# Query and key projections by seven half products in place of eight, block sums on GpSimd, filler steps laid out anew

## The chip, the core and the metric

The kernel runs on one core of one Trainium2 chip. The metric is the device time of one execution, in microseconds. A core has TensorE (PE, matmuls into the PSUM), VectorE (DVE), ScalarE (ACT), GpSimd (POOL) and a queue processor SP that issues transfers; they run beside each other and wait for each other by semaphores. In the profile PEld is TensorE's weight load, which overlaps its matmuls.

## The reference

Causal self-attention with 16 heads of 32 channels, a normalisation, a mixture of eight experts of which each token uses one, and a second normalisation:

```python
Q, K, V = x @ W_Q.T, x @ W_K.T, x @ W_V.T          # x: 8 x 1024 x 512
attn = Q K^T / sqrt(32), causal; probs = softmax(attn)
x = layernorm(x + (probs @ V) @ W_O.T)
probs = softmax(x @ router_w.T + router_b)          # 8 experts
y = (x @ expert_w[top1].T + expert_b[top1]) * max(probs)
out = layernorm(x + y)
```

All inputs are float32 and are multiplied as float32.

## The kernel before

**Rounds and steps.** The 16 heads are taken in groups of four (128 channels) and the eight sequences one after another, which makes 32 rounds (`n`; sequence `b = n // 4`, group `g = n % 4`). A round has nine steps (`u`). In each step TensorE does, in this order: the scores of one block of queries and keys for four heads (`exps`, lines 745 and 751); one unit of "maxima" for the round that is one and a third ahead (`maxima`, line 635: score blocks from which VectorE takes each row's extreme at line 645); a filler; small extra matmuls, where there are any; and the values (`values`, line 787: probabilities times V). ScalarE turns the scores into exponentials (line 757) and, as room allows, takes the exponentials that give each row its sum (`exp_sums`, line 687). GpSimd cuts the diagonal blocks of the probabilities (line 761, `affine_select`), at steps 0, 1, 2, 4 and 6 of a round: two in steps 1, 2 and 4, one in 0 and 6. The values of a step need that.

**Fillers.** A filler is a projection: 512 input channels in four chunks of 128, each times four groups of 32 output channels, into one PSUM bank. Each round needs four of them for the queries and keys of round `n + 2` (`project_qk`, two halves of the sequence times two matrices, line 572), and four others: output projections of the previous sequence (`output`, line 842), or value projections of the next one (`project_v`, line 600), or, for the first sequence, small products for the router. Nine steps have eight fillers, so one of the other four is cut in two halves of two chunks (`in_halves`), with a copy out for each half: fillers stand in steps 0 to 8, with the halves in steps 5 and 7 (`HALVES_AT`). In a half step the fourth maximum is taken only after the filler was copied out.

**Order.** All engines' orders are written out by hand, instruction by instruction. VectorE's order in a step is: the maxima; one entry of the list `later`, if there is one; the filler's copy out (line 579, 581, 595 or 823); a fourth maximum that was left; the copies of the extras; the addition of the values to the context (lines 803 and 807); statistics of a finished output row block (lines 830, 831). `later` holds the normalisations of the first layer norm (`normalize`, line 858, 128 x 512 elements read and written in SBUF, followed by a store of `x1` on SP) and the two additions that finish a sequence's router logits (lines 936 and 937). Four normalisations follow each half sequence of output projections, which fill the first and second rounds of the next sequence; so they stand in steps 0 to 3 of the second round, and in steps 0, 2, 3 and 4 of the third, whose step 1 has the logits.

**Banks.** Of the eight PSUM banks one (`ps_f`) holds the filler and then the first head's scores of the next step, three (`ps_s`) hold the other heads' scores, and four (`ps_m`) go round among four maxima, extras and values. So the next scores wait for the filler's copy out.

**Inputs.** A sequence's x, transposed, stands in SBUF in two tiles of 512 tokens. The next sequence's tiles are loaded at step 7 of the second round (`load_x`, line 537), once the last reader is through. SP issues these loads, the fetches of h (x again, for the residual, line 815) and the stores of `x1` (line 861) in one queue. At the start the query weights and the first tile come in four chunks each, then the whole of the key weights, then the second tile.

**After the rounds.** Routing sorts tokens by expert, in small pieces of VectorE and GpSimd work (line 289 on GpSimd for the first six sequences, in rounds 26 to 30), and the experts follow, some 312 us.

The queries are scaled when they are copied out:

```python
                    if name == "wq":
                        nc.vector.tensor_scalar_mul(dst[n][:, cols], ps, -scale)
                    else:
                        nc.vector.tensor_copy(dst[n][:, cols], ps)
```

## Time and profile before

| what | value |
|---|---|
| median of three executions | 2213.53 us (2211.68 to 2213.75) |
| the profiled execution | 2210.15 us, its span 2208.1 us |
| TensorE, VectorE, ScalarE, GpSimd busy | 97%, 72%, 70%, 17% of the span |
| lead-in before the first round | 83.8 us |
| a round of sequences 1 to 5 | 57.31 to 57.74 us |
| one query or key projection on TensorE | 3.46 us to the next operation |
| granted TensorE clock | 0.997 |

The span is the time from the first to the last instruction of the profiled execution; some 2 us lie around it. A group's row names the line, engine and operation, output and inputs with their shapes, the number of instructions, then busy time and the mean of one in nanoseconds, then the idle time just before and what ended it. A timeline's row gives start and duration in microseconds, and in brackets the idle time before and its releaser; a matmul of float32 appears as two records.

### The profile page before, as it was taken

To read this page: it belongs to the slowest core of one execution; us is meant where nothing else is said; L and a number is where in the kernel's file an instruction comes from. 1 tells how busy PE (TensorE), PEld (TensorE's weight loads), DVE (VectorE), ACT (ScalarE), POOL (GpSimd) and SP (SyncE) were. 2 spreads that over 40 slices of the span, in tenths; PEclk is the share of its full clock that TensorE was granted. 3 is DMA by queue.
4 is the path that set the end of the run, shared out by engine and by line. 5 is a ranking of instruction groups with operands and counts; after the bars stand their busy time and mean duration, and the time that the engine had idled before them with its cause. 6 is when DMAs were issued, how large, how long until landed. Compare 5 with 4: busy or idle time off the path is not lost. (4 is left out here: it accounts for less than half of the span.)

```text
span 2208.1 us, 52961 instructions
## 1 busy us (share of the span) xinstructions
PE 2146.4 (97%) x20731; PEld 846.0 (38%) x20731; DVE 1581.3 (72%) x4867; ACT 1544.1 (70%) x2979; POOL 370.8 (17%) x485
## 2 busy tenths in 40 slices
PE   8998999999999999999999999999999988999998
PEld 2333333333333333333333333333333333344444
DVE  4666667766777677766776677667778876478766
ACT  2688777777777777887777877777777777243443
POOL 0000001100100010100110001001000224255554
PEclk9999999999999999999999999999999999999999
DMA  3001000110011002100120002000101031343432
GB/s 115 1 1 64 1 2 16 63 40 1 10 70 40 2 2 73 45 2 1 35 83 1 2 35 82 2 2 35 54 7 44 11 120 64 133 153 124 134 127 84
DMA packets 45736, 103.82 MB, mean 47 GB/s; under 512 B 5998, under 2 KB 5998, under 8 KB 45360
## 3 DMA queue, kind: packets, MB, share of 16 engines
q1 hardware_dynamic: 33456, 65.02, 8.3%
q0 software_dynamic: 11360, 35.40, 5.1%
q8 instruction: 164, 2.69, 0.5%
q14 instruction: 84, 0.69, 0.1%
q10 hardware_dynamic: 672, 0.02, 0.0%
HBM read 66.87 MB, written 35.39 MB: 46 GB/s over the span
## 5 line engine op out<-in xcount | busy, mean ns | idle before, releaser
L757 ACT ACTIVATE p<-s 128x512 f32<-128x512 f32 x584 | 558.5, 1009 | 422.8 <-PE s L751 422.7
L687 ACT ACTIVATE raw<-raw,low 128x1024 f32<-128x1024 f32 (+7 forms) x1024 | 779.1, 770 | 43.2 <-DVE low L645 43.2
L645 DVE CUSTOM_DVE_ANT_0 raw<-m,wide_mask 128x512 f32<-128x512 f32 (+3 forms) x1024 | 566.8, 587 | 156.0 <-PE m L635 156.0
L572 PE MATMUL f<-big 128*32 128x512 f32 x3968 | 451.4, 595 | 0.7 <-ACT p L757 0.7
L761 POOL TENSOR_SCALAR_AFFINE_SELECT p<-p 128x512 f32<-128x512 f32 x256 | 158.8, 638 | 1427.3 <-ACT p L757 1427.2
L645 DVE CUSTOM_DVE_ANT_0 raw<-m,wide_mask,lowA 128x256 f32<-128x256 f32 (+3 forms) x512 | 275.2, 548 | 136.2 <-PE m L635 136.2
L787 PE MATMUL pv<-p,V 128*32 128x512 f32 (+3 forms) x3072 | 304.0, 488 | 15.9 <-POOL p L761 5.6
L751 PE MATMUL s<-big 32*128 32x512 f32 (+3 forms) x3072 | 313.1, 487 | 0.0
L635 PE MATMUL m<-big 32*128 32x512 f32 (+3 forms) x3072 | 312.6, 486 | 0.3 <-DVE ctx L803 0.3
L435 PE MATMUL y<-big,gT 128*128 x568 | 255.8, 593 | 2.6 <-ACT gT L427 2.6
L600 PE MATMUL f<-big 128*32 128x512 f32 x2048 | 235.9, 596 | 4.2 <-ACT p L757 4.2
L572 PEld LDWEIGHTS f<-big 128*32 128x32 f32 x3968 | 116.2, 109 | 284.8 <-issue 222.6
L842 PE MATMUL f<-wo,ctx 128*32 128x512 f32 x1920 | 221.1, 596 | 2.6 <-ACT p L757 2.6
L635 PEld LDWEIGHTS m<-big 32*128 32x128 f32 x3072 | 171.7, 185 | 85.9 <-issue 59.0
L687 ACT ACTIVATION_READ_ACCUMULATOR raw<-raw,low 128x1 f32 x1024 | 200.1, 195 | 0.0
L807 DVE TENSOR_TENSOR ctx<-pv,ctx 128x512 f32<-128x512 f32 (+2 forms) x256 | 150.7, 589 | 38.6 <-PE pv L787 37.6
L787 PEld LDWEIGHTS pv<-p,V 128*32 128x32 f32 x3072 | 93.9, 110 | 188.7 <-issue 141.2
L751 PEld LDWEIGHTS s<-big 32*128 32x128 f32 x3072 | 142.8, 185 | 19.1 <-issue 14.6
L745 PE MATMUL s<-mT,ones_b 3*128 3x512 bf16 (+3 forms) x1536 | 134.0, 327 | 12.7 <-DVE mT L712 3.8
L435 PEld LDWEIGHTS y<-big,gT 128*128 128x128 f32 x568 | 102.4, 190 | 105.8 <-issue 101.9
L453 ACT ACTIVATE yrstd<-ymv,eps 128x1 f32<-128x1 f32 x71 | 20.9, 295 | 152.4 <-DVE ymv L451 134.5
L745 PEld LDWEIGHTS <-ones_b 3*128 3x128 bf16 x1536 | 46.5, 91 | 202.2 <-issue 190.7
(205 smaller groups left out, 1603.6 us busy)
## 6 DMA issues: line engine op xcount, KB each, us to landing
h<-in_x SPq DMA_DIRECT2D x64, 256.0 KB, 3.6
x<-h SPq DMA_DIRECT2D x64, 256.0 KB, 2.0
big<-in_xT SPq DMA_DIRECT2D x15, 1024.0 KB, 7.3
big<-in_ewT SPq DMA_DIRECT2D x8, 1024.0 KB
bias<-in_eb SPq DMA_DIRECT2D x1, 2048.0 KB
g<-x,r_gat POOLq DMA_INDIRECT x71
out<-g,r_sca POOLq DMA_INDIRECT x71
big<-in_xT SPq DMA_DIRECT2D x4, 256.0 KB, 5.7
```

The source lines that it names most:

```text
L435: nc.tensor.matmul(y_ps, lhsT=gT[:, k, :], rhs=big[:, bass.ds(e, 1), k, :].rearrange("p a o -> p (a o)"), start=(k == 0), stop=(k == NK - 1),)
L572: nc.tensor.matmul(ps, lhsT=w_sb[name][:, k, g * P : (g + 1) * P][:, m], rhs=xT_sb[b, c][:, k, :], start=start, stop=stop,)
L600: lambda ps, k, m, start, stop: nc.tensor.matmul(ps, lhsT=xT_sb[b, c][:, k, o : o + P][:, m], rhs=w_sb["wv"][:, k, :], start=start, stop=stop,
L635: nc.tensor.matmul(tiles[h][:, at : at + c1 - c0], lhsT=Q[n][r, qt * P : (qt + 1) * P], rhs=K[n][r, c0:c1], start=True, stop=True,)
L645: nc.vector.tensor_tensor_reduce(out=raws[n, h][:, to : to + w], in0=tiles[h][:, at : at + w], in1=wide_mask[:, 640 - w :] if last else wi ...
L687: nc.scalar.activation(a[:, to : to + w], a[:, to : to + w], AF.Exp, scale=-1.0, bias=low[n][:, qt, h : h + 1], accum_out=sums[n][:, qt, h ...
L745: nc.tensor.matmul(tiles[h][:, at : at + w], lhsT=ones_b[r, :], rhs=mT[n][r, q0 : q0 + w], start=True, stop=False,)
L751: nc.tensor.matmul(tiles[h][:, at : at + w], lhsT=K[n][r, j * P : (j + 1) * P], rhs=Q[n][r, q0 : q0 + w], start=False, stop=True,)
L757: nc.scalar.activation(p[:, hs], scores, AF.Exp, scale=-1.0)
L761: nc.gpsimd.affine_select(out=p[:, :, at : at + P], in_=p[:, :, at : at + P], compare_op=ALU.is_ge, fill=0.0, base=0, pattern=[[0, HG], [1 ...
L787: nc.tensor.matmul(ps[h * HD : h * HD + HD, parts[c][1] - w : parts[c][1]], lhsT=V[b, j][:, ch : ch + HD], rhs=p[:, h, at : at + w], start ...
L842: lambda ps, k, m, start, stop: nc.tensor.matmul(ps, lhsT=ctx_of(b * NG + k, qt * P, P)[:, m], rhs=w_sb["wo"][:, k, :], start=start, stop= ...
```

## The change

Half of the input channels of x and of the two weight matrices make a 2 x 2 problem: x has two halves of the sequence by two halves of the channels, the weights two halves of the channels by the two matrices. Strassen's method (in Winograd's form) does it with seven products of half the channels in place of eight, and sums of blocks.

- The class `seven` holds a round's products. GpSimd makes the sums of x blocks (`s`, 128 x 1024) and of weight blocks (`t`, 128 x 256), in one buffer each that is rewritten in place: `begin` after step 5 of the round before, `second` behind step 0, `third` behind step 1 and `fourth` behind step 3; `third` also adds two finished blocks (128 x 512). GpSimd stays in program order, so selects of later steps stand behind the sums.
- Products stand in steps 0 (two), 1, 2 (two), 3 and 5, the whole other fillers in steps 4, 6, 7 and 8. The second product of a step takes a bank of `ps_m`. They are copied or added into Q and K by VectorE, eight instructions of 128 x 512 in a round where there were four; the other fillers are not cut any more, which takes one copy out away.
- Rounds 0 and 1 are projected as before; then GpSimd scales both weight matrices in SBUF by the square root of the scale, once, in the lead-in.
- Short steps are now 1, 3 and 5; small extra matmuls move to steps 3 and 5; the next sequence's load moves to step 3 of the second round, after `fourth`.
- The first weights are loaded by columns: those of the first group before the first tile, the others after the second.
- `mT` (the turned maxima) has one buffer in place of two, the second half's context six in place of seven, and round 30 takes the buffer of `s` for its context.

```diff
-            def load_w(name, w, k0=0, k1=NK):
+            def load_w(name, w, o0=0, o1=D):
...
+                def sum(self, out, a, op, b):
+                    nc.gpsimd.tensor_tensor(out, a, b, op)
+
+                def begin(self):
+                    (a11, a12), (a21, a22) = self.x
+                    (b11, b12), (b21, b22) = self.w
+                    self.sum(self.s, a21, ALU.add, a22)
+                    self.sum(self.t[0], b12, ALU.subtract, b11)
+                    self.sum(self.t[1], b22, ALU.subtract, self.t[0])
+
+                def second(self):
+                    self.sum(self.s, self.s, ALU.subtract, self.x[0][0])
+                    self.sum(self.t[0], self.t[1], ALU.subtract, self.w[1][0])
+
+                def third(self):
+                    self.sum(self.s, self.x[0][1], ALU.subtract, self.s)
+                    self.sum(self.k[1], self.k[1], ALU.add, self.q[1])
+                    self.sum(self.t[1], self.w[1][1], ALU.subtract, self.w[0][1])
+
+                def fourth(self):
+                    self.sum(self.s, self.x[0][0], ALU.subtract, self.x[1][0])
+
+                def product(self, x, w, out):
+                    def mm(ps, k, m, start, stop):
+                        nc.tensor.matmul(ps, lhsT=w[:, k][:, m], rhs=x[:, k, :], start=start, stop=stop)
+
+                    return project(mm, out, ks=range(2))
...
+                    return {
+                        0: [self.product(self.s, self.t[0], copy(k[1])), self.product(a11, b11, copy(q[0]))],
+                        1: [self.product(self.s, self.t[1], add((q[1], q[0])))],
+                        2: [
+                            self.product(a12, b21, add((q[0], q[0]))),
+                            self.product(a22, self.t[0], add((q[1], q[1]), op=ALU.subtract)),
+                        ],
+                        3: [self.product(self.s, b22, add((k[0], k[1])))],
+                        5: [self.product(self.s, self.t[1], add((q[1], q[1]), (k[1], k[1])))],
+                    }, {0: self.second, 1: self.third, 3: self.fourth}
...
-            HALVES_AT = (NU - 4, NU - 2)
+            HALVES_AT = (1, 3, 5)
+            WHOLE_AT = (4, 6, 7, 8)
...
-                mT[n] = small.tile([P, S], BF16, tag="mT", bufs=2, name=f"mT_{n}")
+                mT[n] = small.tile([P, S], BF16, tag="mT", bufs=1, name=f"mT_{n}")
...
-            CTX_BUFS = (NG + 1, NG + 3)
+            CTX_BUFS = (NG + 1, NG + 2)
...
+            load_w("wq", wqT, 0, P)
             for k in range(NK):
                 load_x(0, 0, k, k + 1)
-                load_w("wq", wqT, k, k + 1)
-            load_w("wk", wkT)
+            load_w("wk", wkT, 0, P)
             load_x(0, 1)
+            load_w("wq", wqT, P, D)
+            load_w("wk", wkT, P, D)
...
+                if t == 2 * NC:
+
+                    nc.gpsimd.tensor_scalar_mul(w_sb["wq"], w_sb["wq"], -math.sqrt(scale))
+                    nc.gpsimd.tensor_scalar_mul(w_sb["wk"], w_sb["wk"], math.sqrt(scale))
+                    made_next = seven(2)
+                    made_next.begin()
...
+                made = {u: [f] for u, f in zip(range(HALF, NU) if n == NP - 1 else WHOLE_AT, fill)}
+                behind = {}
                 if n + 2 < NP:
...
+                    halves, behind = made_next.steps()
+                    made.update(halves)
...
+                    if u in behind:
+                        behind[u]()
...
+                    if u == HALVES_AT[-1] and n + 3 < NP:
+                        made_next = seven(n + 3)
+                        made_next.begin()
```

More of the change, by code (lines that the diff above doesn't have):

```diff
@@ L489, in attention @@
             pool2 = lambda name, bufs: st2.enter_context(tc.tile_pool(name=name, bufs=bufs))
-            vp, prob = pool2("v", 1), pool2("prob", 2)
+            vp, prob, sums_p = pool2("v", 1), pool2("prob", 2), pool2("sums", 1)
             NG = NH // HG
@@ L527, in attention @@
             xT_sb, Q, K, V, H, MV, ctxT, mT = {}, {}, {}, {}, {}, {}, {}, {}
-            def load_w(name, w, k0=0, k1=NK):
+            def load_w(name, w, o0=0, o1=D):
                 nc.sync.dma_start(
-                    out=w_sb[name][:, k0:k1], in_=w.rearrange("(k p) o -> p k o", p=P)[:, k0:k1]
+                    out=w_sb[name][:, :, o0:o1], in_=w.rearrange("(k p) o -> p k o", p=P)[:, :, o0:o1]
                 )
@@ L583, in project_qk, with __init__, steps, add @@
                 return project(mm, out)
+            class seven:
+                def __init__(self, n):
+                    b, g = divmod(n, NG)
+                    cols = slice(g * P, (g + 1) * P)
+                    self.x = [[xT_sb[b, c][:, k : k + 2, :] for k in (0, 2)] for c in range(NC)]
+                    self.w = [[w_sb[name][:, k : k + 2, cols] for name in ("wq", "wk")] for k in (0, 2)]
+                    self.s = sums_p.tile([P, 2, 512], F32, tag="s", name=f"xs_{n}")
+                    self.t = [sums_p.tile([P, 2, P], F32, tag=f"t{i}", name=f"ws_{n}_{i}") for i in range(2)]
+                    q, k = big[:, 5 + n % 3, 0:2], big[:, 5 + n % 3, 2:4]
+                    Q[n], K[n] = [a.rearrange("p k t -> p (k t)") for a in (q, k)]
+                    self.q, self.k = [q[:, c] for c in range(NC)], [k[:, c] for c in range(NC)]
+                def sum(self, out, a, op, b):
[19 more added lines that the diff above has]
+                    return project(mm, out, ks=range(2))
+                def steps(self):
+                    (a11, a12), (a21, a22) = self.x
+                    (b11, b12), (b21, b22) = self.w
+                    q, k = self.q, self.k
+                    def add(*to, op=ALU.add):
+                        def out(ps):
+                            for dst, a in to:
+                                nc.vector.tensor_tensor(dst, a, ps, op)
+                        return out
+                    def copy(dst):
+                        return lambda ps: nc.vector.tensor_copy(dst, ps)
+                    return {
[8 more added lines that the diff above has]
+                    }, {0: self.second, 1: self.third, 3: self.fourth}
@@ L796, in add @@
                     for c, (w, end) in parts.items():
-                        if (n, c) not in ctxT:
+                        if (n, c) == (NP - 2, 1):
+                            if (n, c) not in ctxT:
+                                ctxT[n, c] = sums_p.tile([P, 2, 512], F32, tag="s", name="ctx_more")[:, 0]
+                        elif (n, c) not in ctxT:
                             ctxT[n, c] = cp.tile([P, 512], F32, tag=f"ctx{c}", bufs=CTX_BUFS[c], name=f"ctx_{n}_{c}")
@@ L983, in attention @@
                 b, g = divmod(n, NG)
-                fill = []
-                if n + 2 < NP:
-                    fill += [project_qk(n + 2, c, name) for c in range(NC) for name in ("wq", "wk")]
                 if b == B - 1 and g < NG - 1:
                     first_qt, end_qt = ((0, HALF), (HALF, HALF + 2), (HALF + 2, NQT))[g]
-                    todo = [(output, b - 1, qt) for qt in range(first_qt, end_qt)]
+                    fill = [output(b - 1, qt) for qt in range(first_qt, end_qt)]
                 elif g < 2:
-                    todo = [(output, b - 1, qt) for qt in range(g * HALF, (g + 1) * HALF) if b]
-                    if not b:
-                        fill += [f for k in range(g * 2, g * 2 + 2) for f in router_of_ctx(k)]
+                    if b:
+                        fill = [output(b - 1, qt) for qt in range(g * HALF, (g + 1) * HALF)]
+                    else:
+                        fill = [f for k in range(g * 2, g * 2 + 2) for f in router_of_ctx(k)]
                 elif b + 1 < B:
-                    todo = [(project_v, b + 1, i) for i in range((g - 2) * HALF, (g - 1) * HALF)]
+                    fill = [project_v(b + 1, i) for i in range((g - 2) * HALF, (g - 1) * HALF)]
                 else:
-                    todo = [(output, b, qt) for qt in range(HALF)]
-                if len(fill) + len(todo) == NU - 1 and todo:
-                    a, c, d, e = [f(*args) for f, *args in todo[:1]] + [in_halves(*todo[1])] + [f(*args) for f, *args in todo[2:]]
-                    fill += [a, c[0], d, c[1], e]
-                else:
-                    fill += [f(*args) for f, *args in todo]
-                slots = range(NU)
-                if n == NP - 1:
-                    slots = range(HALF, NU)
-                elif n == NP - 3:
-                    slots = (0, 1, 2, 3, 5, 7)
-                made = dict(zip(slots, fill))
-                assert len(made) == len(fill)
+                    fill = [output(b, qt) for qt in range(HALF)]
+                made = {u: [f] for u, f in zip(range(HALF, NU) if n == NP - 1 else WHOLE_AT, fill)}
+                behind = {}
+                if n + 2 < NP:
+                    halves, behind = made_next.steps()
+                    made.update(halves)
                 small_ones = {u: [] for u in range(NU)}
@@ L1016, in attention @@
                         small_ones[late].append(lambda ps: logits_part(b - 1, [NG - 1], False, ps))
-                    small_ones[late].append(lambda ps: logits_part(b, [0, 1], True, ps))
+                    small_ones[HALVES_AT[2]].append(lambda ps: logits_part(b, [0, 1], True, ps))
                 elif g == 1:
                     if b:
-                        small_ones[HALVES_AT[0]].append(lambda ps: turn_logits(b - 1, ps))
+                        small_ones[HALVES_AT[2]].append(lambda ps: turn_logits(b - 1, ps))
                     small_ones[late].append(lambda ps: logits_part(b, [2, 3], True, ps))
@@ L1031, in attention @@
                     exps(n, u)
-                    short = u in HALVES_AT and len(made) == NU
+                    short = u in HALVES_AT and n + 2 < NP
                     left = maxima_at(t, HG - 1 if short else HG)
@@ L1036, in attention @@
                         later.pop(0)()
-                    extra, f = small_ones[u], made.get(u)
+                    extra, fs = small_ones[u], made.get(u, [])
                     piece = None
@@ L1044, in attention @@
                     if n == NP - 1:
-                        outs.append(values(*divmod(n * NU + u - 1, NU), ps_f if u % 2 and not f else ps_m))
-                    if f:
-                        out, rest = f(bank(f"f_{n}_{u}", ps_f))
+                        outs.append(values(*divmod(n * NU + u - 1, NU), ps_f if u % 2 and not fs else ps_m))
+                    rest = None
+                    for i, f in enumerate(fs):
+                        out, rest = f(bank(f"f_{n}_{u}_{i}", ps_m if i else ps_f))
                         outs.append(out)
@@ L1058, in attention @@
                     exp_sums(t)
-                    if f and rest:
+                    if rest:
                         rest()
                     after_maxima(t)
+                    if u in behind:
+                        behind[u]()
                     if piece:
```

## The prediction

> **What bounds the kernel now.** I read the page's busy shares first, then the groups of instructions, then the timelines of TensorE and VectorE in one round, then places where GpSimd and VectorE meet.

> ```profile
> span 2208.1 us, 52961 instructions
> ...
> PE 2146.4 (97%) x20731; PEld 846.0 (38%) x20731; DVE 1581.3 (72%) x4867; ACT 1544.1 (70%) x2979; POOL 370.8 (17%) x485
> ...
> L572 PE MATMUL f<-big 128*32 128x512 f32 x3968 | 451.4, 595 | 0.7 <-ACT p L757 0.7
> ...
> L761 POOL TENSOR_SCALAR_AFFINE_SELECT p<-p 128x512 f32<-128x512 f32 x256 | 158.8, 638 | 1427.3 <-ACT p L757 1427.2
> ```

> TensorE is the bound (97%, 62 us idle), and L572, the work the change shrinks, hardly waits. GpSimd is nearly free. The second view is TensorE's timeline: start, duration, operation.

> ```profile
> 600.62 0.34 PE L745 MATMUL s<-mT,ones_b 3*128 3x384 bf16 x4
> ...
> 601.76 1.04 PE L635 MATMUL m<-big 32*128 32x512 f32 x8
> 602.74 3.64 PE L572 MATMUL f<-big 128*32 128x512 f32 x32
> 606.20 1.05 PE L787 MATMUL pv<-p,V 128*32 128x384 f32 x16
> 607.19 0.29 PE L745 MATMUL s<-mT,ones_b 3*128 3x256 bf16 x4
> ...
> 640.79 1.92 PE L842 MATMUL f<-wo,ctx 128*32 128x512 f32 x16
> 642.53 1.05 PE L906 MATMUL e<-big,rwx 128*32 128x256 f32 x16
> ```

> A step is scores, maxima, a filler and values. A whole filler holds TensorE from 602.74 to 606.20, 3.46 us; a half from 640.79 to 642.53, 1.74. From step start to step start the four rounds of a batch take 57.42, 57.74, 57.31 and 57.31 us, the same in every batch from 1 to 5. VectorE in the same step:

> ```profile
> 602.93 0.69 DVE L645 CUSTOM_DVE_ANT_0 raw<-m,wide_mask 128x512 f32<-128x512 f32 x1 [1.50 <-PE m L635]
> ...
> 605.38 0.54 DVE L858 TENSOR_SCALAR h<-h,mv,rstd 128x512 f32<-128x512 f32 x1
> 606.45 0.69 DVE L581 COPY big<-f 128x512 f32<-128x512 f32 x1 [0.52 <-PE f L572]
> ```

> Four maxima start 0.61 us apart, then a normalisation (L858), then the filler is copied out; the next scores need that bank. Now the same normalisation beside GpSimd's routing work:

> ```profile
> 1753.12 1.48 POOL L289 TENSOR_TENSOR r_each<-r_hot,r_values 128x288 bf16<-128x288 bf16 x2
> ...
> 1753.15 0.92 DVE L858 TENSOR_SCALAR h<-h,mv,rstd 128x512 f32<-128x512 f32 x1
> ...
> 1753.99 0.68 DVE L579 TENSOR_SCALAR big<-f 128x512 f32<-128x512 f32 x1
> ...
> 1754.72 0.34 PE L745 MATMUL s<-mT,ones_b 3*128 3x384 bf16 x4 [0.84 <-DVE big L579]
> ```

> L858 takes 0.92 in place of 0.54: it ends 0.28 after the first of the two sums (1753.12 to 1753.79). The copy is late, and TensorE idles 0.84. Two more L858 that fall inside such sums take 1.03 and 0.62, a third, when its sum was just ending, 0.555; L645, which overlaps GpSimd hundreds of times, keeps its 0.69. So a GpSimd sum stops this kind of VectorE instruction until it ends.

> **The change part by part.** T is a step's first score matmul, and rounds 0 to 29 of the 32 make products.

> *Fewer products.* Fifteen halves in place of sixteen: -1.74 a round.

> *Step 8.* Steps 7 and 8 take 13.11 together (5.62 + 7.49 or 5.19 + 7.92), and in the first round of a batch 13.22; a half, a whole (6.50), the turn of the maxima (0.55) and the extras (0.86, 0.43 or 1.29) sum to 12.70, 12.27 and 13.13. The rest, on the mean 0.44, comes from ScalarE's table loads and VectorE's splitting after a short step 7. Step 7 becomes whole: -0.44.

> *Step 1 becomes a half.* Its values would be ready at T+3.86, but scores take until T+1.40 to reach ScalarE, exponentials end at T+3.34, and the first of its two selects (L761, 0.64) ends at T+4.11: +0.34. Before, whole fillers covered it.

> *Step 5 becomes a half with two copies out.* Three maxima end at T+4.08, two additions end at T+5.37, scores are due at T+4.79: +0.63 in the third and fourth round of a batch; in the others an extra matmul covers it. Mean +0.32. Step 2 has two additions and two context parts on VectorE; the maxima's fourth bank comes some 0.1 late.

> Together -1.74 - 0.44 + 0.34 + 0.32 + 0.10 = -1.42 a round, -43 over 30.

> *Start.* The first four projections need 2.5 MB in place of 4. They now begin at 5.04, 13.20 (a 1.35 wait for the key weights follows a 0.80 one), 17.64 and 22.09; undisturbed they are 4.45 apart. That would put the first maxima near 22.2 and not 25.66: -3.4, between 0 (rows of 512 bytes arrive no sooner) and -3.7.

> *GpSimd's sums.* No row has 128x1024 with two inputs. Lower end: the select's rate, 0.638 for 512, gives 1.27. Upper: L289, 0.668 for 288, gives 2.38. L289 is the same operation; its start-to-start of 0.627 gives 2.23, so I take 2.3. The small ones (256) are 0.6. Four large, four small and one of 512 make 12.7 us a round beside selects of 5.1, in 56: GpSimd is no bound. The selects queued behind them are due 3.4 after a step's start; the sums begin 3.9 to 4.1 after one (when the product has read the old sum) and end before the next select, the longest chain (third: 2.3 + 1.2 + 0.6 behind step 1) by 3.2 in step 2. The price is nothing up to some 2.6 per large sum; beyond, step 2's values still have 1.4 of slack.
> [...]

> *Normalisations against those sums.* L858, and the two small additions of the logits, run in steps 0 to 3 (4) of the second and third rounds of a batch: 13 rounds with products (seven second, six third). L858 reaches its data 0.26 after its start (0.54 less 0.28).
> Step 0: the sum runs T+4.07 to 6.37, L858 is there at T+5.2: it ends at 6.65, the copy at 7.26, scores start at 7.31 in place of 6.51: +0.80.
> Step 1: the product ends 2.90 after the maxima's start m, so the sum starts at m+3.00 (0.08 to 0.13 from a release to GpSimd, L836 and L761); a delayed L289 (0.85 for 0.67, beside L858) shows that it needs its data 0.15 later, m+3.15. L858 starts at m+1.17+3x0.61 = m+3.01 and needs data at m+3.27. GpSimd wins by 0.12: L858 ends at T+6.72, the addition at 7.33, scores at 7.38 in place of 5.20: +2.18. In third rounds the logits' additions stand there; if the first slips in, the second does not.
> Step 3: the same, scores at T+7.32 for 5.62, and 0.5 in step 4 because VectorE's rest leaves its banks late: +2.2.
> Steps 2 and 4 have no sum at that time. That is 5.2 x 12.5 (round 29 is partly held by ScalarE, so half) = +65; ends 0 and +80.
> [...]

> *Routing.* In rounds 26 to 29 VectorE's routing pieces meet the sums too: +4 (0 to 10).

> *At nothing.* The input load moves from step 7 to step 3 of the second round, in SP's queue behind four stores of x and ahead of three fetches of h. It waits for the fourth sum (T+6.4), lands within 8.5, and is read some 16 later: the cover is 1 us; gone, it would cost step 6's select, 1 to 2 us seven times. The fetched h is used two steps on. Scaling the weights and the first sums fall into the lead-in, before anything reads them. One buffer less for maxima and context: the reads end a step before the next write.

> Sum: -43 - 3.4 + 65 + 4 = +23 on the profiled execution's 2210.15, so 2233. That execution is 3.4 under the median; against it I say 2236.

> **The rivals.**
> *VectorE gets in first in steps 1 and 3* (ends faster). For it: 0.12 us decides. Then step 0 (0.80 x 13), the logits' step (2.2 x 6) and 0.3 x 7 remain, 26 in place of 65: 2194, 2197 against the median. One race of the two: step 1's saves 1.9 x 6.5 (the logits' steps stay blocked), step 3's 2.2 x 12.5, so 2224 or 2209.
> *Sums short or harmless.* At 1.27 step 0 has no collision, step 1 costs 1.15, step 3 0.67: 2194. With none, 2168. Against it: L289's rate and the blocked L858.
> *GpSimd late as well.* Sums over 2.9 delay selects too; at 3.2 the collisions cost 35 more and selects some 15: 2286. Only an unforeseen slowness of fp32 speaks for it.

> **How the numbers follow.** Forecast (2222 to 2252) 0.51; one race 0.13; VectorE first 0.14; short or harmless sums 0.15; over 2252 0.07. The range 2180 to 2252 leaves out 0.07 above and about as much below (sums without any collision). Within 0.2% (4.4 us, what a measurement here can tell) falls part of the one-race case: 0.05, with 0.05 of it faster and 0.03 slower. Faster: 0.14 + 0.15 + 0.05 = 0.34. Slower: 0.51 + 0.07 + 0.03 = 0.61. The likeliest case's own range is 2222 to 2252.

> **What would show it.** L572's matmul records fall and the products appear at 8 matmuls each (16 records). Undisturbed rounds (first and fourth of a batch) take near 56; second and third near 61, with TensorE waiting for VectorE before the scores of steps 1, 2 and 4, and L858's mean well over 0.54. First maxima near 22. It is wrong if L858 stays near 0.55 (then faster), or if GpSimd's large sums are far from 2.3.

## The result and the profile after

The changed kernel takes 2223.76 us (median of five executions, 2222.88 to 2229.41). The kernel before took 2213.53 on the same chip (2210.77 to 2214.16). The ratio is 1.0057, with a 95% interval of 1.0041 to 1.0072: slower by 0.6%. The forecast was 2236, slower, in a range of 2180 to 2252.

The page of the changed kernel, busy shares and two groups of instructions (line, engine, operation, tiles and shapes, then busy time and mean of one in ns, then the idle time ahead of it and its releaser):

```profile
span 2222.0 us, 52374 instructions
...
PE 2119.3 (95%) x20251; PEld 837.2 (38%) x20251; DVE 1670.6 (75%) x4960; ACT 1546.9 (70%) x2979; POOL 793.0 (36%) x757
...
L604 POOL TENSOR_TENSOR xs<-big 128x1024 f32<-128x1024 f32 x60 | 144.3, 2406 | 357.6 <-PE f L627 357.6
...
L818 PE MATMUL s<-mT,ones_b 3*128 3x512 bf16 (+3 forms) x1536 | 132.8, 329 | 58.8 <-DVE big L640 34.1
```

TensorE lost 27 us of work (2146.4 to 2119.3) and the span still grew by 13.9, so it now waits 41 us more. L818, the scores at the start of a step (L745 before), waits 58.8 us, most of it for L640, the additions by which VectorE takes a product out of PSUM. The groups with their shapes kept apart show what came late ahead of L640:

```profile
L935 DVE TENSOR_SCALAR h<-h,mv,rstd 128x512 f32<-128x512 f32 x64 | 60.5, 945 | 2.3 <-POOL rstd L913 2.3
...
L1014 DVE TENSOR_TENSOR logits<-logits,rb_sb 128x64 f32<-128x64 f32 x8 | 14.1, 1769 | 0.3
```

L935 is the normalisation (L858 before, 0.54 undisturbed): its mean is now 0.945. L1014, the second addition of the logits, has 64 elements a row and takes 1.77 on the mean.

Where the 13.9 us of span come from, from one score to the next: lead-in -1.2, rounds 0 to 3 -7.1, rounds 4 to 23 +15.4, rounds 24 to 31 +6.4, the experts behind them +0.5. The twenty rounds 4 to 23 (sequences 1 to 5) are the measure below. In the kernel before each repeats within 0.01 us from sequence to sequence; in the changed kernel second rounds vary from 58.00 to 60.34 and third ones from 59.99 to 63.77.

| kernel | time, us | ratio to before (95%) | 1st | 2nd | 3rd | 4th | rounds 4 to 23 | rounds 24 to 31 |
|---|---|---|---|---|---|---|---|---|
| before | 2213.5 | | 57.42 | 57.74 | 57.31 | 57.31 | 1148.9 | 440.0 |
| changed | 2223.8 | 1.0057 (1.0041 to 1.0072) | 56.29 | 58.48 | 62.13 | 55.96 | 1164.3 | 446.4 |
| normalisations moved | 2175.3 | 0.9833 (0.9817 to 0.9850) | 56.29 | 56.48 | 56.27 | 55.96 | 1125.0 | 436.2 |
| normalisation on ScalarE | 2186.7 | 0.9881 (0.9864 to 0.9897) | 56.29 | 56.48 | 56.68 | 55.97 | 1127.1 | 443.1 |
| no sums | 2180.2 | 0.9868 (0.9848 to 0.9889) | 56.28 | 57.10 | 57.00 | 56.02 | 1132.0 | 436.3 |
| no sums, normalisations moved | 2170.8 | 0.9815 (0.9798 to 0.9833) | 56.28 | 56.47 | 56.27 | 56.02 | 1125.2 | 432.4 |
| eight halves, no sums | 2218.8 | 1.0036 (1.0022 to 1.0051) | 57.66 | 58.52 | 58.08 | 57.10 | 1156.8 | 441.6 |
| sums in halves | 2205.5 | 0.9977 (0.9967 to 0.9986) | 56.29 | 58.36 | 59.27 | 55.96 | 1149.5 | 446.0 |
| sums 640 + 384 | 2196.6 | 0.9938 (0.9922 to 0.9955) | 56.35 | 57.48 | 58.36 | 55.96 | 1140.8 | 441.3 |
| logits back in step 1 | 2202.2 | 0.9962 (0.9950 to 0.9974) | 56.29 | 56.48 | 59.83 | 55.96 | 1142.8 | 446.7 |

Single rounds are means over sequences 1 to 5 of the profiled execution. The median of the kernel before was 2210.8, 2211.7 and 2210.9 on the chips of the experiments, and each ratio is against its own.

A third round in which all goes wrong is round 6, which takes 63.77. VectorE's timeline at its steps 0, 1 and 3 (start, duration, engine, line, operation):

```profile
418.01 1.61 DVE L935 TENSOR_SCALAR h<-h,mv,rstd 128x512 f32<-128x512 f32 x1
...
424.42 0.62 DVE L1013 TENSOR_TENSOR logits<-logits,rstd 128x64 f32<-128x64 f32 x1
425.07 2.28 DVE L1014 TENSOR_TENSOR logits<-logits,rb_sb 128x64 f32<-128x64 f32 x1
427.27 0.68 DVE L640 TENSOR_TENSOR big<-big,f 128x512 f32<-128x512 f32 x1
...
440.26 2.74 DVE L935 TENSOR_SCALAR h<-h,mv,rstd 128x512 f32<-128x512 f32 x1
```

GpSimd's timeline in the same steps:

```profile
416.94 2.39 POOL L604 TENSOR_TENSOR xs<-xs,big 128x1024 f32<-128x1024 f32 x1
...
423.74 1.22 POOL L834 TENSOR_SCALAR_AFFINE_SELECT p<-p 128x512 f32<-128x512 f32 x2 [3.53 <-ACT p L830]
424.93 2.34 POOL L604 TENSOR_TENSOR xs<-big,xs 128x1024 f32<-128x1024 f32 x1
...
440.34 2.37 POOL L604 TENSOR_TENSOR xs<-big 128x1024 f32<-128x1024 f32 x1 [7.66 <-PE f L627]
```

Each VectorE instruction ends just after the GpSimd instruction that it met, by an amount that the author estimates to be the time that its own data take: the normalisations 0.29 later (419.62 after 419.33, 443.00 after 442.71), the logits' additions 0.08 later (425.04 after the second select's 424.96, 427.35 after 427.27). L640, which waits behind them, keeps its length. TensorE's next scores wait for it, in step 2 for 2.51:

```profile
428.00 0.29 PE L818 MATMUL s<-mT,ones_b 3*128 3x256 bf16 x4 [2.51 <-DVE big L640]
```

### The profile page after: what moved, and what is told of

It reads as the page before. It is cut to its first block, busy times and chain, and to the rows that moved or that the text cites. A ratio compares the mean times of both kernels' runs of the same rounds, so it can differ in the third digit from the quotient of the medians.

```text
span 2222.0 us, 52374 instructions
## 1 busy us (share of the span) xinstructions
PE 2119.3 (95%) x20251; PEld 837.2 (38%) x20251; DVE 1670.6 (75%) x4960; ACT 1546.9 (70%) x2979; POOL 793.0 (36%) x757
## 5 line engine op out<-in xcount | busy, mean ns | idle before, releaser
L717 DVE CUSTOM_DVE_ANT_0 raw<-m,wide_mask 128x512 f32<-128x512 f32 (+3 forms) x1024 | 571.3, 586 | 145.1 <-PE m L707 145.0
L717 DVE CUSTOM_DVE_ANT_0 raw<-m,wide_mask,lowA 128x256 f32<-128x256 f32 (+3 forms) x512 | 273.1, 548 | 128.6 <-PE m L707 128.6
L707 PE MATMUL m<-big 32*128 32x512 f32 (+3 forms) x3072 | 326.1, 495 | 0.8 <-DVE ctx L884 0.8
L604 POOL TENSOR_TENSOR xs<-big 128x1024 f32<-128x1024 f32 x60 | 144.3, 2406 | 357.6 <-PE f L627 357.6
L672 PE MATMUL f<-big 128*32 128x512 f32 x2048 | 234.0, 597 | 0.0
L707 PEld LDWEIGHTS m<-big 32*128 32x128 f32 x3072 | 183.2, 188 | 88.4 <-issue 63.3
L818 PE MATMUL s<-mT,ones_b 3*128 3x512 bf16 (+3 forms) x1536 | 132.8, 329 | 58.8 <-DVE big L640 34.1
L627 PE MATMUL f<-xs,ws 128*32 128x512 f32 x1440 | 173.1, 598 | 0.4
L884 DVE TENSOR_TENSOR ctx<-pv,ctx 128x384 f32<-128x384 f32 (+2 forms) x250 | 146.6, 587 | 29.8 <-PE pv L861 27.8
L818 PEld LDWEIGHTS <-ones_b 3*128 3x128 bf16 x1536 | 45.3, 91 | 249.8 <-issue 203.6
```

The source lines that it names most:

```text
L627: nc.tensor.matmul(ps, lhsT=w[:, k][:, m], rhs=x[:, k, :], start=start, stop=stop)
L672: lambda ps, k, m, start, stop: nc.tensor.matmul(ps, lhsT=xT_sb[b, c][:, k, o : o + P][:, m], rhs=w_sb["wv"][:, k, :], start=start, stop=stop,
L707: nc.tensor.matmul(tiles[h][:, at : at + c1 - c0], lhsT=Q[n][r, qt * P : (qt + 1) * P], rhs=K[n][r, c0:c1], start=True, stop=True,)
L717: nc.vector.tensor_tensor_reduce(out=raws[n, h][:, to : to + w], in0=tiles[h][:, at : at + w], in1=wide_mask[:, 640 - w :] if last else wi ...
L818: nc.tensor.matmul(tiles[h][:, at : at + w], lhsT=ones_b[r, :], rhs=mT[n][r, q0 : q0 + w], start=True, stop=False,)
```

## The experiments

Two explanations stood against each other. In A a GpSimd sum stops these VectorE instructions until it ends (the lock, in the words below; 2.74 us in place of 0.54 at 440.26 above). In B VectorE has too much to do in the new layout (75% busy, with more copies out of PSUM in half steps) and would be late without any lock.

**Normalisations moved.** The entries of `later` may only stand in steps 2, 4, 6, 7 and 8, where no large sum runs at their time; the logits' additions come first among them. Every instruction is still executed.

```diff
-                            later.insert(1, lambda: finish_logits(b))
+                            later.insert(0, lambda: finish_logits(b))
...
-                    if later:
+                    if later and (n + 2 >= NP or u in (2, 4, 6, 7, 8)):
```

> The normalisations and the logits' additions of the second and third rounds wait for steps 2, 4, 6, 7 and 8, where no large GpSimd sum runs at that moment; every instruction is still there. Theory A (a GpSimd sum stops these VectorE instructions until it ends): second rounds fall from 58.0 to about 56.3 us, third ones from about 62.9 to 56.0, the L935 group's mean returns to 0.54, the step of 8.15 us at a lower clock goes with the idle time ahead of it, and the time is 2223.8 - 7 x 1.9 - 6 x 6.9 = 2169 (2162 to 2178), ahead of both kernels. Theory B (VectorE simply has too much to do in the new layout): the 0.54 us costs as much in another step, 2215 to 2224.

It took 2175.26 us (2171.68 to 2176.30): 1.7% faster than the kernel before, the fastest of the kernels here that compute everything. Its groups:

```profile
L935 DVE TENSOR_SCALAR h<-h,mv,rstd 128x512 f32<-128x512 f32 x64 | 34.7, 542 | 1.2 <-POOL rstd L913 1.2
...
L1014 DVE TENSOR_TENSOR logits<-logits,rb_sb 128x64 f32<-128x64 f32 x8 | 2.2, 271 | 0.3
```

The normalisation is back at 0.542 and the logits' addition at 0.271. Second and third rounds take 56.48 and 56.27, and the slow steps 2 are gone. So the place of these few instructions decides the sign of the whole change. It doesn't yet separate A from B, because a whole step can also hide 0.54 us that a half step can't.

**No sums.** GpSimd's sums are left out, and the products multiply the blocks as they are; the normalisations stay where the change has them.

```diff
-                    self.s = sums_p.tile([P, 2, 512], F32, tag="s", name=f"xs_{n}")
-                    self.t = [sums_p.tile([P, 2, P], F32, tag=f"t{i}", name=f"ws_{n}_{i}") for i in range(2)]
+                    self.s, self.t = self.x[1][0], [self.w[0][1], self.w[1][1]]
...
-                    nc.gpsimd.tensor_tensor(out, a, b, op)
+                    pass
```

> All of GpSimd's sums are left out and the seven products multiply blocks as they are (Q and K are then not the reference's). Normalisations stay where the change has them. Theory A: second and third rounds fall to 56.3 and 56.0, L935's mean is 0.54: 2223.8 - 55 = 2169, less some 0.3 x 28 where step 1 waits for its values no longer than its selects: 2158 to 2172. Theory B: the sums are innocent, 2215 to 2224.

2180.16 us (2178.96 to 2187.38), some 11 more than expected, since B has a share: second rounds stay at 57.10 and not 56.3. Their step 1 takes 5.62, exactly as in the second rounds of the changed kernel with all its sums, against 5.17 in a first or fourth round. There it is VectorE's 0.54 us in a half step that counts, not a lock. Step 3 takes 5.73, also as in the changed kernel, against 5.21, but 0.43 of that is TensorE's own: the extra matmuls of step 3 are 16 records in second and third rounds and 8 in the others, and the step takes 5.64 with the normalisation on ScalarE (below). Step 0 is 6.48 without sums and 7.42 with them: that is the lock.

**No sums, normalisations moved.** Both edits above.

> Normalisations moved and the sums left out as well (Q and K are not the reference's). Theory A, and nothing else wrong with the sums: within 5 us of the kernel with moved normalisations, 2168 to 2177, rounds of the middle batches at 56.3, 56.5, 56.3, 56.0 in both. Rival (the sums also cost through late selects or memory): 2165 or less, with shorter first and fourth rounds.

2170.79 us (2168.45 to 2172.90), and rounds 4 to 23 take 1125.2 against 1125.0 with the sums: GpSimd's sums, 13.8 us a round by the groups of the kernel with moved normalisations, cost nothing once nothing meets them. The four kernels split the twenty rounds:

- seven products in the new layout, no collision, against before: 1125.0 - 1148.9 = -23.9
- the normalisations and the logits standing in half steps, without sums: 1132.0 - 1125.2 = +6.8
- the sums on top of that: 1164.3 - 1132.0 = +32.3

Together +15.2; measured +15.4. The +32.3 can be built from the steps: ten steps 0 at 0.94 (9.4), five steps 1 of third rounds at 7.73 against 5.68 (10.3), three lost races in step 3 at 2.2 with what step 4 inherits (6.6), and four steps 2 at a lower clock at 1.6 (6.3): 32.6.

**Normalisation on ScalarE.** One activation with scale and bias in place of VectorE's instruction, in the same step; GpSimd works out the bias from four values a row.

```diff
-                nc.vector.tensor_scalar(
-                    h, h, MV[b][:, qt, 0:1], rstd[b][:, qt : qt + 1], ALU.subtract, ALU.mult
+                nc.scalar.activation(
+                    h, h, AF.Identity, scale=rstd[b][:, qt : qt + 1], bias=moved[b][:, qt : qt + 1]
                 )
```

> The normalisation stays in its step, but ScalarE does it (one activation with scale and bias; GpSimd makes the bias, 4 values a row). The logits' two additions stay on VectorE in step 1 of the third rounds. Theory A: steps 0 and 3 of second and third rounds return to 6.5 and 5.2 us, step 1 of second rounds too, step 1 of third rounds stays near 7.5: 2223.8 - 13 x 0.94 - 7 x 0.45 - 9 = 2199 (2190 to 2208). Theory B (VectorE's load): it falls by what is taken off VectorE where it is late, 13 rounds x 4 x 0.54 at most in part, so steps 0, 1 and 3 shorten by 0.54 each at most: 2205 to 2222, and step 1 of third rounds falls below 7.2.

2186.72 us (2180.25 to 2187.96), better than expected, and steps 0 and 3 return to 6.48 and 5.64 (5.2 had been expected of step 3, without its larger extra matmuls). ScalarE isn't stopped: its 64 normalisations take 0.81 on the mean, and the one that starts at 415.25 takes 0.81 with a large sum running from 415.78 to 418.17. The miss is step 1 of third rounds, 5.62 where 7.5 was expected. The logits' additions were still in place, and met this:

```profile
422.29 0.22 DVE L1017 TENSOR_TENSOR logits<-logits,rstd 128x64 f32<-128x64 f32 x1
422.55 0.55 DVE L1018 TENSOR_TENSOR logits<-logits,rb_sb 128x64 f32<-128x64 f32 x1
```

GpSimd's two selects came 0.2 us later in the step than in the changed kernel, so the first addition slipped ahead of the second select and the second one was under way when the sum started at 422.99. A phase of 0.2 us decides over 2 us.

**Logits back in step 1.** The kernel with moved normalisations, with only the logits' additions of the third rounds put back:

```diff
-                    if later and (n + 2 >= NP or u in (2, 4, 6, 7, 8)):
+                    if later and (n + 2 >= NP or u in (2, 4, 6, 7, 8) or (g, u) == (2, 1)):
```

> The kernel with the moved normalisations, with one thing put back: the logits' two additions of the third rounds stand in step 1 again. If the second addition meets the third sum, step 1 of third rounds takes 7.7 and not 5.2 us, with 2.5 us in which TensorE waits: 2175 + 6 x 2.5 = 2190. If such a wait makes the granted clock fall in the step behind it, step 2 takes near 8.1 in most third rounds: 2198. If the phase of the selects lets both additions in ahead of the sum (as in the run with the normalisation on ScalarE), step 1 takes 5.6 and the time is 2178.

2202.17 us (2200.55 to 2211.29). All third rounds of sequences 1 to 5 have a step 1 of 7.75, 2.58 more: one 64-element addition held by one sum. Behind it, step 2 takes 7.97, 6.57, 8.19, 7.98 and 6.57 in them, where 6.50 is usual. Windows of that kernel over step 2 of rounds 6 and 10 (start and end, length, busy time of each engine, granted clock, DMA) show which ones are long (the second one leaves out the step's first 0.2 us):

```profile
424.69:432.66 7.97, 7.97 (x88) 4.05 (x89) 5.37 (x22) 5.58 (x12) 3.17 (x4) 0.81 0.00 0
654.00:660.30 6.30, 6.30 (x88) 2.95 (x82) 5.17 (x22) 5.16 (x11) 2.99 (x4) 1.00 0.00 0
```

In the long ones TensorE works without a pause (7.97 of 7.97) at a granted clock of 0.81 on the mean; in the short ones the clock is 1.00, after the same wait. Five additions thus cost 17.8 us over the twenty rounds, 12.9 in the wait and 5 in the clock. The rest of the difference to 2175.3 lies in rounds 24 to 31, 10 us longer, where routing work stands in the same queues; that part wasn't taken apart.

**Sums in halves.** Each large sum is cut into two instructions of 128x512.

```diff
-                    nc.gpsimd.tensor_tensor(out, a, b, op)
+                    w = out.shape[-1] // (2 if len(out.shape) == 3 else 1)
+                    for k in range(2 if len(out.shape) == 3 and w == 256 else 1):
+                        o, y, z = [v[:, k] if w == 256 else v for v in (out, a, b)]
+                        nc.gpsimd.tensor_tensor(o, y, z, op)
```

> Each large sum becomes two instructions of 128x512 (1.28 each, as the 512 sum in the same profile), all else stays as the change has it. Theory A with the lock held per instruction and given to VectorE between two of them: step 0 of second and third rounds falls from 7.42 to about 6.5 us (the first half ends near T+5.35, before the normalisation's data are due), step 1 of third rounds from 7.73 to 6.6, step 3's worst case from 7.47 to 6.4, and with less idle time ahead of it step 2 loses its slow case: 2223.8 - 12 - 7 - 5 - 8 = 2192 (2183 to 2206). Rival: the next half is queued at once and VectorE does not get in between, then all stays, 2222 to 2230.

2205.53 us (2203.85 to 2211.20). Step 1 of third rounds falls to 6.66 and no step 2 is slow, as expected from a lock held for one instruction. Step 3 is 5.64 to 5.74 in every one of them. Step 0 stays at 7.43, which was not expected, and step 4 of second and third rounds grows from 6.73 to 7.08, which wasn't taken apart. VectorE's normalisation and GpSimd's two halves in step 0 of round 6, each engine's timeline (the two halves stand in one row, and the trace has the second one starting 0.06 us after the normalisation):

```profile
415.69 1.63 DVE L938 TENSOR_SCALAR h<-h,mv,rstd 128x512 f32<-128x512 f32 x1
```

```profile
414.50 2.53 POOL L607 TENSOR_TENSOR xs<-xs,big 128x512 f32<-128x512 f32 x2
```

VectorE started first and was still held until the second half ended. That fits an estimate from the two times that the prediction had read from the kernel before (a normalisation needs its data 0.26 after its start, a GpSimd sum 0.15): GpSimd goes first if it starts less than 0.11 after VectorE.

**Sums of 640 + 384.** A test of that number: the second piece now starts later.

```diff
+                        for cut in (slice(0, 640), slice(640, 1024)):
+                            o, y, z = [v[:, cut] for v in flat]
+                            nc.gpsimd.tensor_tensor(o, y, z, op)
```

> Large sums in two pieces of 640 and 384 elements in place of 512 and 512. Law to be tested: the GpSimd piece goes first if it starts less than about 0.11 us after the VectorE instruction, otherwise VectorE does. With equal halves the second half started 0.06 after the normalisation in step 0 and won. A first piece longer by 0.3 us puts the second 0.36 after the normalisation's start: VectorE goes first there, the normalisation takes 0.6 to 0.7 and not 1.63, step 0 of second and third rounds 6.5 and not 7.43. Step 1 of third rounds waits for the longer first piece, 6.65 + 0.3 = 6.95. Time: 2205.5 - 13 x 0.9 + 6 x 0.3 = 2196 (2190 to 2202). If VectorE doesn't get in between the pieces, step 0 stays at 7.4 and the time is 2205 or more.

2196.57 us (2194.83 to 2199.74). Step 0 falls to 6.60 in every second and third round, step 1 of third rounds is 6.93. Again step 0 of round 6:

```profile
416.95 0.79 DVE L941 TENSOR_SCALAR h<-h,mv,rstd 128x512 f32<-128x512 f32 x1
```

The second piece started 0.46 after the normalisation, which was held only by the rest of the first piece (0.79 in place of 1.63).

**Eight halves.** The new layout and loads, with eight half products, their plain copies and additions, and no sums.

```diff
-                        0: [self.product(self.s, self.t[0], copy(k[1])), self.product(a11, b11, copy(q[0]))],
-                        1: [self.product(self.s, self.t[1], add((q[1], q[0])))],
+                        0: [self.product(a11, b11, copy(q[0])), self.product(a21, b11, copy(q[1]))],
+                        1: [self.product(a12, b21, add((q[0], q[0])))],
...
-                        5: [self.product(self.s, self.t[1], add((q[1], q[1]), (k[1], k[1])))],
+                        5: [self.product(a21, b12, copy(k[1])), self.product(a22, b22, add((k[1], k[1])))],
```

> The new layout of the steps, the new loads, and eight half products with their plain copies and additions in place of seven and the sums; right in its result. Against the kernel without sums it has one half product more in each of 30 rounds, 1.74 us: 2169 + 52 = 2221 (2210 to 2226). If it comes out near 2213.5 or below, the layout itself is worth something and the eighth product is partly free; near 2230 or above, the layout costs what the product saves.

2218.82 us (2216.07 to 2221.01). Against the kernel without sums the eighth product costs 1156.8 - 1132.0 = 24.8 in twenty rounds, 1.24 a round and not 1.74. A half step 5 with two additions doesn't end sooner than VectorE: in third and fourth rounds it takes 5.41 without the eighth product and 6.48 with it.

**Old loads.** The changed kernel with the first loads in the order and shapes of before.

```diff
-            load_w("wq", wqT, 0, P)
             for k in range(NK):
                 load_x(0, 0, k, k + 1)
-            load_w("wk", wkT, 0, P)
+                nc.sync.dma_start(out=w_sb["wq"][:, k : k + 1], in_=wqT.rearrange("(k p) o -> p k o", p=P)[:, k : k + 1])
+            load_w("wk", wkT)
             load_x(0, 1)
-            load_w("wq", wqT, P, D)
-            load_w("wk", wkT, P, D)
```

> The changed kernel with the order and the shapes of the first loads as before (whole weight rows, interleaved with the input chunks). If the new loads are worth 0.5 to 1.2 us, as the wait for the key weights says (1.35 before, the copy's 0.8 after), the second projection waits for its weights again, about 0.5 longer than the copy, and the first maxima start near 25.7, where the new loads gave 23.5 to 25.6; the whole time (2222 to 2230) can't show it. If they are worth the 3.4 of the prediction, the first maxima start at 27 or later.

One execution took 2226.54 us. The first maxima start at 26.80, in between the two expectations. With the new loads they started at 23.48 to 25.62 in ten profiles (24.68 on the mean), with the old ones at 25.66 and 26.80. So the loads bring some 1.5 us, with a scatter as large. TensorE's timeline in the lead-in of the old loads and of the kernel with halved sums, whose first projection never waits:

```profile
8.95 4.24 PE L572 MATMUL wq<-big 128*32 128x512 f32 x24 [2.17 <-DMA big<-in_wqT]
14.33 3.64 PE L572 MATMUL wk<-big 128*32 128x512 f32 x32 [1.14 <-DMA big<-in_wkT]
```

```profile
5.13 5.04 PE L572 MATMUL wq<-big 128*32 128x512 f32 x32 [5.13 <-DMA big<-in_xT]
11.00 3.64 PE L572 MATMUL wk<-big 128*32 128x512 f32 x32 [0.82 <-DVE big L579]
```

With the new loads the key projection waits for the copy alone, 0.82. But the first 32 matmul records take 5.04 to 6.79 even where no wait interrupts them, and the next 32 take 3.64. The traces of the kernel before and of the changed one show where: four records follow four every 0.82 to 0.85 us, where nothing interrupts them, until the trace's first record of the granted clock (at 10.44 before, 9.19 in the changed kernel), and every 0.43 to 0.45 behind it. With halved sums that record begins at 7.91, and windows ahead of it and behind it (as in the windows above, the count in brackets is of records) have TensorE at little more than half the pace and then at the full one:

```profile
5.13:7.91 2.78, 2.77 (x16) 0.52 (x20) 0.00 (x0) 0.00 (x0) 0.00 (x0) 1.00 0.96 274
7.91:10.17 2.26, 2.26 (x24) 0.43 (x16) 0.00 (x0) 0.00 (x0) 0.00 (x0) 1.00 1.08 382
```

The 1.00 in the first of them says only that no clock is on record there.

**Logits first in round 26.** An attempt at a better end: moved normalisations, and the logits' additions of round 26 in its step 0.

```diff
-                    if later and (n + 2 >= NP or u in (2, 4, 6, 7, 8)):
+                    if later and (n + 2 >= NP or u in (2, 4, 6, 7, 8) or (n, u) == (NP - 6, 0)):
```

> The moved normalisations, but the logits' additions of round 26 go first, in its step 0, so that the routing work starts two steps earlier than in the run before. It beats that run if the 6 us by which its last two rounds are longer come from routing work that was pushed back: 2172 (2167 to 2176); step 0 of round 26 should take up to 0.9 more.

2178.99 us (2178.42 to 2180.83), ratio 0.9855 (0.9839 to 0.9872): no gain. Rounds 4 to 23 are the same (1125.0), and the last eight take 439.3 against 436.2. Starting the routing earlier only puts it into the way elsewhere: round 26 takes 61.47 for 58.42, round 28 63.14 for 59.81, rounds 30 and 31 together 89.0 for 92.5.

## Why the prediction was right, and where its steps were not

The verdict and the mechanism held: the sums stop VectorE's normalisations, and this costs more than the eighth product. The total was 12 us too high, and several of its terms were off.

That the total came out inside the likeliest case's 2222 to 2252 is in part luck. VectorE won step 1 of second rounds and seven of ten races in step 3. At the prediction's own prices (1.9 x 6.5 and 0.7 of 2.2 x 12.5) these take 32 from the 2236 and leave 2204, faster than before. What made up for it were terms that the sum had lower or not at all: VectorE's own work in half steps (6.8 in twenty rounds), the clock (6.3), and smaller savings by the products and the loads.

*Fewer products, steps 8, 1, 5 and 2: -1.42 a round.* Measured without collisions -1.20 (23.9 in twenty rounds). Undisturbed rounds came out at 56.29 and 55.96, forecast near 56.

*Start, -3.4.* Measured -1.2 in the profiled execution, about -1.5 from all profiles. The step that failed is "undisturbed they are 4.45 apart": it took the pace of later projections for the first, whose matmuls run 1.4 to 3.15 us longer in all, at half the pace up to the first record of the clock.

*Sums of 2.3.* The groups of the changed kernel and of the one with moved normalisations show 2.36 to 2.41 for 1024 elements, 1.29 to 1.32 for 512, and 0.74 to 0.81 for 256. All sums together are 13.8 us a round and not 12.7.

*Step 0, +0.80.* Measured +0.94 in all ten second and third rounds, and 7.42 in step 0 for the 7.31 of the working.

*Step 1, +2.18 in thirteen rounds.* Wrong in its working: it let the sum start when the product ended, and forgot that two selects stand ahead of it in GpSimd's queue until T+4.7. So the sum starts 0.51 after the normalisation. The normalisation passes, held only by a select (0.82), and step 1 takes 5.62, which it would take without sums too: +0.45 in second rounds. The aside that "in third rounds the logits' additions stand there; if the first slips in, the second does not" was the part that came true, at +2.56.

*Step 3, "GpSimd wins by 0.12", +2.2.* The bound, an estimated 0.11 after the normalisation's start, was right (the runs put it between 0.09 and 0.17), and the start was wrong. The start of the sum had been put 0.10 after the product's end; it is 0.18 in all ten second and third rounds. The product had been put at 2.90 after the maxima's start; it ends at 2.90 to 2.91 in rounds 6, 14 and 17, where GpSimd starts 0.08 to 0.09 after the normalisation and wins. In the seven others of rounds 4 to 23 it ends at 2.99 to 3.06, and GpSimd starts 0.17 to 0.24 after the normalisation and loses; the step then takes 5.73 to 5.80, 0.1 to 0.2 over its 5.64 instead of 2.2. So the rival in which VectorE wins this race came true seven times in ten. Why the product ends later in these rounds stays open.

*Steps 2 and 4 have no sum.* True, but step 2 paid all the same, through the clock.

*Collisions, +65 in all, and routing, +4.* Moving the normalisations saves 48.5 us (2223.8 to 2175.3). Of the 39.3 that go in rounds 4 to 23, 6.8 are VectorE's own work in half steps and 6.3 the clock, neither of which the working had. What routing adds in rounds 26 to 29 wasn't separated from the rest; rounds 24 to 31 take 446.4 with the collisions and 436.2 with the normalisations moved.

The rival "sums short or harmless" is out by the 32.3 us that go with them, and "GpSimd late as well" by the list of waits, where TensorE waits 2.8 us in all for the selects. "VectorE first in steps 1 and 3" was half true, and the kernel with moved normalisations shows what was left to gain.

## What to carry to other kernels

Before work is given to an idle engine, look at what its instructions stop on the others while they run: here some 14 us a round of GpSimd sums cost nothing or 1.6 us a round, depending on the steps in which sixty-four instructions of half a microsecond and sixteen smaller ones stood. Move the victims into steps without such work, or cut the blocking instruction where they arrive, before judging the change by its total. And when two engines' start times differ by a tenth of a microsecond, work out each one's queue, not only its data, and give both outcomes.

## What the runs showed of the hardware that was not expected

*Who goes first.* In rounds 4 to 23 of the changed kernel every normalisation that met a large sum obeyed one bound. Where GpSimd started up to 0.09 us after VectorE (0.08 to 0.09 in step 3 of rounds 6, 14 and 17) or ahead of it (by 1.06 in ten steps 0), VectorE waited for its end and took 2.73 to 2.74 or 1.61 to 1.62. Where GpSimd started 0.17 or more after it (0.17 to 0.24 in seven steps 3, 0.51 in five steps 1), VectorE went first and the sum was the longer one, 2.53 to 2.60 in place of 2.36 to 2.40. Step 0 of round 6 with the sums cut agrees: 0.06 after, the normalisation was held (1.63), and 0.46 after, only by the piece before (0.79). In round 10 of the changed kernel, from the two engines' timelines:

```profile
672.70 0.54 DVE L935 TENSOR_SCALAR h<-h,mv,rstd 128x512 f32<-128x512 f32 x1
```

```profile
672.88 2.59 POOL L604 TENSOR_TENSOR xs<-big 128x1024 f32<-128x1024 f32 x1 [6.26 <-PE f L627]
```

So one blocks the other for a whole instruction (2.74 for 0.54), but within a tenth of a microsecond the later starter won, so the order that counts is that of a later point than the start in the trace.

*Size doesn't matter.* An addition of 64 elements a row, 0.27 alone, took 2.28: a short victim waits for the end of the sum as a large one does (2.74). The additions out of PSUM (L640) and the maxima (L717) kept their 0.68 and 0.69 beside the same sums.

*The clock after a wait.* In nine of twelve third rounds (five of six in the changed kernel, four of six with the logits put back) step 2, behind the wait of 2.5 us in step 1, takes 8.0 to 8.2 for 6.5 at a granted clock of 0.79 to 0.81. That is a mean: windows of the changed kernel over the whole step 2 of rounds 6 and 10, then, for round 6, over its parts and the stretch before, and last over a stretch ahead of step 2 of round 10 (columns as above: start and end, length, busy time of each engine, granted clock, DMA):

```profile
427.95:436.12 8.17, 8.12 (x88) 3.78 (x87) 5.82 (x22) 5.79 (x12) 3.18 (x4) 0.79 0.08 29
...
662.05:668.62 6.57, 6.57 (x92) 3.15 (x92) 5.44 (x22) 5.23 (x11) 3.18 (x4) 1.00 0.00 2
...
425.62:429.03 3.41, 1.03 (x24) 0.92 (x26) 3.41 (x5) 0.00 (x0) 2.65 (x2) 1.00 0.00 0
429.03:432.44 3.41, 3.41 (x32) 1.79 (x28) 1.34 (x7) 2.75 (x3) 1.93 (x4) 0.50 0.00 0
432.44:436.12 3.68, 3.68 (x44) 1.08 (x36) 3.40 (x13) 3.04 (x10) 0.24 (x1) 1.00 0.17 65
...
657.73:661.14 3.41, 1.80 (x24) 0.46 (x17) 3.38 (x6) 1.69 (x6) 3.37 (x3) 1.00 0.02 5
```
